# Edge attention on one core: register reads issued a run ahead, two-batch one-hots, wider windows, and 13 more gathered columns taken on chip

## The chip, the core and the metric

The kernel runs on one core of a Trainium2 chip. The metric is device time in microseconds (us) of one launch; the time shown is the median of three runs. TensorE is called PE, its weight loads PEld, VectorE DVE, ScalarE ACT, GpSimd POOL and SyncE SP, as in the profile.

## The reference, cut to what matters

A graph layer over N = 6250 nodes and E = 206,250 edges sorted by destination, 8 heads of 16:

```python
Qh, Kh, Vh = h @ WQ, h @ WK, h @ WV          # 6250 x 128, seen as 8 heads of 16
Eh = edge_attr @ WE                          # 206250 x 128
score = einsum('ehd,ehd,ehd->eh', Kh[src], Qh[dst], Eh) / 4
score = exp(clip(score, -5, 5))              # one number per edge and head
wV = segment_sum(Vh[src] * score[:, :, None], dst)
Z  = segment_sum(score, dst)
out = layernorm(h + wV / (Z + 1e-6))
```

## The kernel before, in words

**Tiles and batches.** The edges are cut into NT = 1612 tiles of 128; 4 tiles are a batch (`cut_batches`, L62), 401 full batches and five short ones at the end. From batch 12 on the order of every engine is written out by hand: what the loop at L591 emits is the order in which each engine's instructions stand (`manual_schedule`, L593).

**The rows of K and V.** At the start `table` (L270) computes K and V of all nodes and writes them to the HBM table `kv`, and keeps x transposed on chip in `xT_sb`. `gather` (L410) then fetches, per tile, the 128 rows `kv[src]` by one indirect DMA that POOL issues (L419); up to 12 batches of gathered rows (`GB`) are kept, and the first gather of batch b waits for PE's expansion of batch b - lag(b), where `lag` (L360) falls from 12 to 3.

**Column tiles.** For some tiles the rows are not gathered: their 128 source nodes' columns of x are copied out of `xT_sb` into a tile `xcol` and multiplied by the K and V weights (`project_columns` L394, `place_columns` L404). `column_tiles` (L73) picks 163 last-of-batch tiles, 3 in every 7 batches. Of the 128 columns of such a tile ACT copies 88 (L392, one per instruction, in 11 runs of 8) and DVE 40 (L389, two per instruction, in 5 runs of 8, so 4 instructions a run). The addresses are numbers in `col_at`; before each run `columns` (L369) loads its 8 addresses into registers of that engine (L382, one TENSOR_LOAD, an instruction that the engine's instruction queue carries out itself; the profile shows it as DVEq and ACTq) and the run's copies follow directly. How many runs are due at a batch follows from a linear rule (L375). DVE's runs all stand in one place, after `messages` (L636).

**One batch.** Iteration b emits, for DVE: `kq` of batch b-1 (L481, K rows times Q rows), the one-hot of batch b+2 (`stage_0`, L449, 128 x 4 x 64), `kqe` of b-1 (L484, times the edge projection), the transposed one-hot of b+2 (`stage_0t`, L459, 126 x 512 in bf16), the sum per head `sc` (L487), `msg` of b-2 (L525), the column runs (L389), the clip of `sc` (L490). In four places `fill` (L583) puts one instruction of a Q block (L301) or of a layernorm (L741) between these. For PE: `eps` (L471, edge projection of b, which waits until `kqe` of b-1 has read the one buffer), `qps` (L474, Q rows by the transposed one-hot), blocks that are complete (`finps`, L510), `agg` (L547, sums per node by the one-hot, batch b-2), and the column product (L401). For ACT: half of its column runs, the copy of a complete block (`fin`, L520), the placing of a column product (L408), the two exps of b-1 (L497, L498), the other column runs, the copy of a finished window's sums (L553).

**Windows.** `agg` sums 128-row one-hots: 8 successive tiles share a window, whose two halves of 4 tiles sit in rows 0 to 63 and 64 to 127; two windows share a PSUM tile and are copied out together. When all windows of a pair of 128-node blocks are there, `finish` (L513) adds them with shifted identities on PE (`add_windows`), ACT copies the result to `fin`, and the layernorm goes through `fill`, from `rz` (L749) on.

**Second half of the destinations.** `from_window(1)` (L183), at batch 30, loads `dB_sb` by DMA and DVE's next instruction (L191) uses it.

Of the kernel before, what the change touches and what calls it, by code (L numbers as in the profile page):

```python
# [9 lines left out]
F32 = mybir.dt.float32  # L10
# [7 lines left out]
P = 128  # L18
# [3 lines left out]
B = 4  # L22
G = 4
HW = 64
HALF = 16
# [8 lines left out]
OHB = (3, 5)  # L34
# [17 lines left out]
COLP = (7, 3)  # L52
COLA = (8, 11)
COLV = (8, 5)
COLL = 8
RING = 4096
SUMS = 8
# [22 lines left out]
def pair_of(t):  # L80

    return (t // (2 * G), t // G % 2) if t < LAST else (NT, 1)


def pair_start(k):

    return (2 * k * G * N + NT // 2) // NT - DRIFT


def window_start(t):  # L90
    k, half = pair_of(t)
    return QL * P + HW if k == NT else pair_start(k) + HALF * half

# [7 lines left out]
def edge_attention(ctx: ExitStack, tc: tile.TileContext, x, xT, srcT, srcC, dstT, dstB, dst0, bnd, lo, eaT,  # L101
# [25 lines left out]
    halves = [[cp.tile([P, B, P], F32, name=f"onehot{h}{i}") for i in range(OHB[h])] for h in range(2)]  # L127
# [11 lines left out]
    with ExitStack() as fast:  # L139
# [8 lines left out]
        nc.vector.tensor_scalar(shift[:HW], io_i[:HW], 0, None, op0=ALU.is_equal)  # L148
        nc.vector.tensor_scalar(shift[HW:], io_i[HW:], HALF - HW, None, op0=ALU.is_equal)
        nc.vector.tensor_scalar(ident, io_i[:, P:2 * P], 0, None, op0=ALU.is_equal)  # L150
        for h in range(2):
            for tl in halves[h]:
                nc.vector.memset(tl[:, :, HW - HW * h:P - HW * h], 0.0)
        nc.vector.tensor_copy(iota_f, io2)
        dB_sb = [ip.tile([P, WT * P], I32, name="dB_sb", bufs=1)]
        nc.scalar.dma_start(dB_sb[0][:min(P, NJ)], dstB[:min(P, NJ)])
# [189 lines left out]
        def load_chunk(c):  # L346
            if c in chunks or c * CH >= NT:
                return
            n = min(CH, NT - c * CH) * P
            tl = ep.tile([P, CH * P], F32, name="ea")  # L350
            nc.sync.dma_start(tl[:, :n], eaT[:, c * CH * P:c * CH * P + n])
            chunks[c] = tl
# [12 lines left out]
        used = [0, 0]  # L365

        copied, projected = {}, []

        def columns(eng, b, share=1.0):  # L369
# [6 lines left out]
            while copied.get(engine, 0) < min(due, len(col_batches) * runs):  # L376
                k, j = divmod(copied.get(engine, 0), runs)
                copied[engine] = copied.get(engine, 0) + 1
                if k not in col_tiles:
                    col_tiles[k] = wp.tile([P, P], F32, name="xcol", bufs=4)  # L380
                to, j = col_tiles[k].bitcast(U8), first + j * size
                at = nc.values_load_multi_w_load_instructions(  # L382
                    col_at[k % col_half:k % col_half + 1, k // col_half, j:j + size], engines=(engine,),
                    min_val=XT_AT, max_val=XT_AT + 8 * (N - 1) + 4,
                    skip_runtime_bounds_check_because="edges name nodes")[1]
# [57 lines left out]

        def stage_0(b):
            t0, n = batches[b][0], len(batches[b])
            half = pair_of(t0)[1]
            oh = halves[half][used[half] % OHB[half]]
            used[half] += 1
            nc.vector.tensor_tensor(oh[:, :n, HW * half:HW * half + HW],  # L449
                                    iota_p[:, None, :].to_broadcast([P, n, HW]),  # L450
                                    rel[:, t0:t0 + n, None].to_broadcast([P, n, HW]), op=ALU.is_equal)
            st8[b] = oh, None

        def stage_0t(b):
            t0, n = batches[b][0], len(batches[b])
            oh = st8[b][0]
            ohT = wp.tile([QROWS, B * P], BF16, name="onehotT", bufs=AHEAD + 2)
# [3 lines left out]
            st8[b] = oh, ohT  # L461
# [39 lines left out]
        def windows(q):  # L501

            return [(k, pair_start(k) - q * P) for k in range(min(NT, LAST + 2 * G - 1) // (2 * G))
                    if -HW - HALF < pair_start(k) - q * P < P]

        def add_windows(ps, q, first, stop):

            parts = windows(q)
            for i, (k, s) in enumerate(parts):
                nc.tensor.matmul(ps, shift[:, P - s:2 * P - s], sums[k // 2][:, k % 2],  # L510
                                 start=first and i == 0, stop=stop and i == len(parts) - 1)

        def finish(j):  # L513
# [6 lines left out]
            nc.scalar.copy(fin, ps)  # L520
            pending.append(layernorm(nc, sp, fin, xbs.pop(q), out, q, 2, stores))
# [8 lines left out]
        def stage_c(b):  # L530
            n, g, oh, m = st8.pop(b)
            for i in range(n):
                t = batches[b][i]
                k, half = pair_of(t)
# [5 lines left out]
                u = k if final else k // 2  # L540
                first = u not in aggs
                if first:
                    aggs[u] = psA.tile([P, 2, MW], F32, name="agg")
                    if final:
                        add_windows(aggs[u][:, 0], QL, True, False)
                tail = k == NT if t == NT - 1 else pair_of(t + 1)[0] != k
                nc.tensor.matmul(aggs[u][:, 0 if final else k % 2], oh[:, i, :], m[:, i, :],  # L547
                                 start=not final and t % (2 * G) == 0, stop=tail)
                if tail and final:
                    norms.insert(0, layernorm(nc, sp, aggs.pop(u)[:, :1], xbs.pop(QL), out, QL, 1, stores))  # L550
                elif tail and (k % 2 == 1 or t == LAST - 1):
                    sums[u] = sp.tile([P, 2, MW], F32, name="sum", bufs=SUMS)
                    nc.scalar.copy(sums[u][:, :k % 2 + 1], aggs.pop(u)[:, :k % 2 + 1])  # L553
                    while len(finished) < QL // 2 and all(v // 2 <= u for v, _ in windows(2 * len(finished) + 1)):
# [262 lines left out]
```

## Time and profile before

| | |
|---|---|
| median of three runs | 1858.12 us (1856.61 to 1858.39) |
| the profiled execution: its own time | 1862.53 us |
| the profiled execution: span, first to last instruction | 1860.7 us |
| granted TensorE clock, mean | 0.922 |
| gathers: from the table kv, from x | 1401, 48 |
| column tiles | 163 |
| moved by DMA | 378.43 MB, mean 203 GB/s |

The page's group lines give line, engine, operation, output<-input, number, busy us and mean ns of one, then the idle time of the engine just before these instructions and what ended it. "Issue" there means that the profile shows nothing that the engine waited for. DVE's and ACT's instructions overlap their neighbours by some 0.08 us, so a mean duration is longer than the step from one start to the next.

### The profile page before, as it was taken

How to read it: one execution, taken by the hardware profiler on the slowest of the kernel's cores; microseconds unless marked ns; L12 is line 12 of the kernel's file. 1: busy time of each engine (PE TensorE's matmuls, PEld its weight loads, DVE VectorE, ACT ScalarE, POOL GpSimd, SP SyncE). 2: the span in 40 equal slices, each digit the busy share in tenths (PEclk: the TensorE clock that was granted, in tenths of full speed). 3: DMA queues.
4: the chain of work that ended last, by engine and by line, in shares of the span. 5: the costliest groups of instructions: out<-in, count | busy, mean ns of one | idle time of the engine just before them, and what ended most of it. 6: DMA issues, size and time to landing. Idle time of an engine off the chain costs nothing.

```text
span 1860.7 us, 48856 instructions
## 1 busy us (share of the span) xinstructions
PE 1330.8 (72%) x9376; PEld 1158.3 (62%) x9376; DVE 1680.8 (90%) x6913; ACT 1632.9 (88%) x15519; POOL 1385.7 (74%) x1456
## 2 busy tenths in 40 slices
PE   6887577677776777776776776766777767666776
PEld 4776466566665666665665665656666656656665
DVE  5589799999999999999999999989998999998987
ACT  2339689899999999999999999999999999998992
POOL 6777677777777777777777777777777777777774
PEclk7998799899999999999999899998898999998998
DMA  9776657667776576677677667667766676667662
GB/s 299 213 230 196 180 173 214 199 203 205 209 215 204 178 238 202 187 219 224 192 210 227 190 198 222 198 185 217 215 207 181 204 222 192 194 197 226 204 195 70
DMA packets 171231, 378.43 MB, mean 203 GB/s; under 512 B 58622, under 2 KB 84556, under 8 KB 170918
## 3 DMA queue, kind: packets, MB, share of 16 engines
q0 software_dynamic: 68768, 186.80, 34.6%
q1 hardware_dynamic: 101010, 187.38, 33.1%
q14 instruction: 237, 1.94, 0.3%
q8 instruction: 76, 1.25, 0.3%
q10 hardware_dynamic: 1140, 1.06, 0.2%
HBM read 360.30 MB, written 14.81 MB: 202 GB/s over the span
## 4 chain that ended last, share of the span: by engine, by line
DVE 43%; PE 11%; DMA 11%; issue 6%; DVEq 5%; POOL 4%; ACT 2%; ACTq 0%; POOLq 0%
DMA kvrows<-kv,src 11%; DVE kqe L484 8%; DVE kq L481 8%; DVE xcol L389 7%; DVE sc L487 5%; DVE msg L525 5%; DVEq L382 5%; PE eps L471 4%; DVE onehot L449 4%; POOL kvrows L419 4%; DVE onehotT L459 3%; PE finps L510 3%; PE agg L547 2%; DVE sc L490 1%; ACT xcol L392 1%
## 5 line engine op out<-in xcount | busy, mean ns | idle before, releaser
L419 POOL DMA_INDIRECT kvrows<-kv,src x1401 | 1338.9, 956 | 434.4 <-issue 305.5
L392 ACT COPY xcol<-xT_sb 128x4 uint8 x14344 | 1442.5, 191 | 44.7 <-issue 37.3
L471 PE MATMUL eps<-we_sb,ea 128*128 128x128 f32 x3224 | 489.5, 298 | 456.6 <-issue 224.0
L471 PEld LDWEIGHTS eps<-we_sb,ea 128*128 128x128 f32 x3224 | 425.8, 205 | 549.8 <-issue 458.4
L547 PE MATMUL agg<-msg,onehot 128*128 128x136 f32 x3224 | 533.9, 313 | 35.8 <-DVE msg L525 24.9
L547 PEld LDWEIGHTS agg<-msg,onehot 128*128 128x128 f32 x3224 | 454.5, 211 | 88.9 <-DVE msg L525 86.5
L389 DVE TENSOR_TENSOR xcol<-xT_sb 128x8 uint8 x3260 | 298.8, 159 | 25.1 <-issue 22.8
L481 DVE TENSOR_TENSOR kq<-kvrows,qps 128x512 f32<-128x512 f32 x406 | 274.4, 676 | 46.5 <-DMA kvrows<-kv,src 25.3
L484 DVE TENSOR_TENSOR kqe<-kq,eps 128x512 f32<-128x512 f32 x406 | 272.9, 672 | 2.5 <-PE eps L471 2.1
L525 DVE TENSOR_TENSOR msg<-kvrows,exp_p 128x512 f32<-128x512 f32 x406 | 272.2, 670 | 2.7 <-ACT exp_p L498 2.6
L487 DVE TENSOR_REDUCE sc<-kqe 128x32 f32<-128x512 f32 x406 | 271.1, 668 | 0.4
L449 DVE TENSOR_TENSOR onehot<-iota_p,dst_sb 128x256 f32<-128x256 f32 x406 | 167.3, 413 | 3.2 <-PE agg L547 3.2
L474 PE MATMUL qps<-qw,onehotT 126*128 126x128 bf16 x1612 | 168.8, 229 | 0.0
L459 DVE TENSOR_SCALAR onehotT<-relb,node 126x512 bf16<-126x512 bf16 x406 | 148.6, 367 | 4.6 <-PE qps L474 3.8
L497 ACT ACTIVATE msg<-sc 128x32 f32<-128x32 f32 x406 | 92.8, 229 | 66.0 <-DVE sc L490 61.7
L474 PEld LDWEIGHTS <-onehotT 126*128 126x128 bf16 x1612 | 134.8, 104 | 8.7
L401 PE MATMUL colkv<-wkv_sb,xcol 128*128 128x256 f32 x326 | 108.7, 418 | 0.0
L490 DVE TENSOR_SCALAR sc<-sc 128x32 f32<-128x32 f32 x406 | 82.2, 202 | 0.2
L510 PE MATMUL finps<-sum,shift 128*128 128x136 f32 x640 | 81.0, 285 | 0.0
L510 PEld LDWEIGHTS finps<-sum,shift 128*128 128x128 f32 x640 | 77.5, 194 | 0.0
L498 ACT ACTIVATE exp_p<-sc 128x32 f32<-128x32 f32 x406 | 74.0, 182 | 0.0
L419 POOL DMA_INDIRECT kvrows<-x,src x48 | 45.9, 955 | 20.6 <-issue 12.8
(76 smaller groups left out, 569.1 us busy)
## 6 DMA issues: line engine op xcount, KB each, us to landing
ea<-eaT SPq DMA_DIRECT2D x201, 512.0 KB
relb<-relD SPq DMA_DIRECT2D x100, 504.0 KB
kvrows<-kv,src POOLq DMA_INDIRECT x1401
qw<-qs SPq DMA_DIRECT2D x202, 31.5 KB
kv<-kvst SPq DMA_DIRECT2D x12, 512.0 KB
qs<-qst SPq DMA_DIRECT2D x48, 96.0 KB
xst<-xT SPq DMA_DIRECT2D x12, 256.0 KB
xb<-x SPq DMA_DIRECT2D x24, 128.0 KB
```

The lines of the kernel that those rows point to most:

```text
L389: eng.tensor_tensor(to[:, 4 * (j + c):4 * (j + c) + 8], *both, op=ALU.bitwise_or)
L392: copy(to[:, 4 * (j + c):4 * (j + c) + 4], xT_bytes[:, ds(at[c] - XT_AT, 4)])
L419: ins = nc.gpsimd.indirect_dma_start(out=g[:k, i, :f], out_offset=None, in_=rows, in_offset=bass.IndirectOffsetOnAxis(ap=src_col(t)[:k], a ...
L449: nc.vector.tensor_tensor(oh[:, :n, HW * half:HW * half + HW], iota_p[:, None, :].to_broadcast([P, n, HW]), rel[:, t0:t0 + n, None].to_bro ...
L471: nc.tensor.matmul(pe[:, i, :], ea[:, i * P:i * P + P], we_sb, start=True, stop=True)
L474: expanded[b] = nc.tensor.matmul(pq[:, i, :], ohT[:, i * P:i * P + P], loaded[t0 // WT], start=True, stop=True)
L481: nc.vector.tensor_tensor(t0[:, :n], g[:, :n, :D], pq[:, :n], op=ALU.mult)
L484: nc.vector.tensor_tensor(t1[:, :n], t0[:, :n], pe[:, :n], op=ALU.mult)
L487: nc.vector.tensor_reduce(sc[:, :n], t1[:, :n].rearrange("p b (h d) -> p b h d", h=H), axis=AX.X, op=ALU.add)
L510: nc.tensor.matmul(ps, shift[:, P - s:2 * P - s], sums[k // 2][:, k % 2], start=first and i == 0, stop=stop and i == len(parts) - 1)
L525: nc.vector.tensor_tensor(m[:, :n, :D].rearrange("p b (h d) -> p b h d", h=H), g[:, :n, D:].rearrange("p b (h d) -> p b h d", h=H), exp_p[ ...
L547: nc.tensor.matmul(aggs[u][:, 0 if final else k % 2], oh[:, i, :], m[:, i, :], start=not final and t % (2 * G) == 0, stop=tail)
```

## The change

- **Addresses.** `columns` keeps a list of loaded runs per engine: before a run's copies it loads the addresses of the run after it, and the copies use the registers that were loaded a run earlier.
- **Columns.** 6 column tiles in every 13 batches (`COLP`); the code's `column_tiles` gives 176 of them (the change's title says 175), against 163. ACT copies 80 columns of each (10 runs of 8), DVE 48 (6 runs). DVE's runs stand after `messages` in even iterations; in odd iterations half are due after `kq` and half after `kqe`, where no one-hot stands any more. `xcol` has 5 buffers instead of 4.
- **One-hots.** One DVE instruction makes the one-hots of two batches (128 x 8 x 64), one the transposed ones (126 x 1024), in every second iteration.
- **Windows.** A window is 16 tiles: its four parts of 4 tiles lie 16 rows apart, which the start of the slice taken from the one-hot buffer does. There are 101 windows' sums of 136 columns, each copied out by itself, and 185 products with a shifted identity in `finish` instead of 320.
- **Blocks.** ACT's copy of a complete block stands behind the two exps of the iteration instead of ahead of them.
- **dB_sb.** The loads go into a buffer of the ring of edge tiles (`ea`). The first is issued when `from_window(0)` first runs instead of among the first loads of ACT's queue; at the second three iterations pass between the load and its first use.

In emitted order, an even iteration of DVE is kq, one-hot, kqe, transposed one-hot, sc, msg, 2 or 3 times (load, 4 copies), clip; an odd one is kq, 1 or 2 times (load, 4 copies), kqe, 1 or 2 times (load, 4 copies), sc, msg, clip; with the fill instructions between as before.

```diff
+QUAD = 4
+STEPS = 16
-OHB = (3, 5)
+OHB = 5
-COLP = (7, 3)
-COLA = (8, 11)
-COLV = (8, 5)
+COLP = (13, 6)
+COLA = (8, 10)
+COLV = (8, 6)
+XCOLS = 5
-SUMS = 8
+SUMS = 9
...
         def from_window(i):
-            if i == len(dB_sb):
-                dB_sb.append(ip.tile([P, WT * P], I32, name="dB_sb", bufs=1))
-                nc.sync.dma_start(dB_sb[i][:k], dstB[a:a + k])
-            d = dB_sb[i]
+            d = ep.tile([P, WT * P], I32, name="dB_sb", tag="ea")
+            (nc.sync if i else nc.scalar).dma_start(d[:k], dstB[a:a + k])
+            if i:
+                yield
+                yield
+                yield
...
         def columns(eng, b, share=1.0):
-            while copied.get(engine, 0) < min(due, len(col_batches) * runs):
+            total = len(col_batches) * runs
+            while copied.get(engine, 0) < min(due, total):
...
-                at = nc.values_load_multi_w_load_instructions(
-                    col_at[k % col_half:k % col_half + 1, k // col_half, j:j + size], engines=(engine,),
+                known = addresses.setdefault(engine, [])
+                while len(known) < 2 and fetched.get(engine, 0) < total:
+                    kf, jf = divmod(fetched.get(engine, 0), runs)
+                    fetched[engine] = fetched.get(engine, 0) + 1
+                    jf = first + jf * size
+                    known.append(nc.values_load_multi_w_load_instructions(
+                        col_at[kf % col_half:kf % col_half + 1, kf // col_half, jf:jf + size], engines=(engine,),
...
+                at = known.pop(0)
...
+        def together(b):
+            t0 = batches[b][0]
+            n = len(batches[b])
+            if n == B and b + 1 < nbat and len(batches[b + 1]) == B and t0 % (2 * B) == 0:
+                return [b, b + 1]
+            return [] if n == B and t0 % (2 * B) else [b]
         def stage_0(b):
-            nc.vector.tensor_tensor(oh[:, :n, HW * half:HW * half + HW],
+            nc.vector.tensor_tensor(tl[:, HW:].rearrange("p (t n) -> p t n", n=P)[:, :n, :HW],
...
+            for i in group:
+                st8[i] = tl, HW + (batches[i][0] - t0) * P - window_of(batches[i][0])[1], None
         def stage_0t(b):
-            ohT = wp.tile([QROWS, B * P], BF16, name="onehotT", bufs=AHEAD + 2)
+            ohT = wp.tile([QROWS, 2 * B * P], BF16, name="onehotT", bufs=3)
...
         def finish(j):
-            nc.scalar.copy(fin, ps)
-            pending.append(layernorm(nc, sp, fin, xbs.pop(q), out, q, 2, stores))
+            def copied_out():
+                nc.scalar.copy(fin, ps)
+                pending.append(layernorm(nc, sp, fin, xbs.pop(q), out, q, 2, stores))
+            blocks_out.append(copied_out)
...
-                    aggs[u] = psA.tile([P, 2, MW], F32, name="agg")
+                    aggs[k] = psA.tile([P, 1, MW], F32, name="agg")
...
-            if b + AHEAD < nbat:
+            if b + AHEAD < nbat and together(b + AHEAD):
                 stage_0(b + AHEAD)
+            elif b < nbat:
+                columns(nc.vector, b, 0.5)
             fill()
             next(steps, None)
-            if b + AHEAD < nbat:
+            if b + AHEAD < nbat and together(b + AHEAD):
                 stage_0t(b + AHEAD)
+            elif b < nbat:
+                columns(nc.vector, b, 1.0)
...
                 weigh(b - 1)
+            while blocks_out:
+                blocks_out.pop(0)()
```

More of the change, by code (lines that the diff above doesn't have):

```diff
@@ L126, in edge_attention @@
     ident = cp.tile([P, P], F32, name="ident")
-    halves = [[cp.tile([P, B, P], F32, name=f"onehot{h}{i}") for i in range(OHB[h])] for h in range(2)]
+    onehots = [cp.tile([P, HW + 2 * B * P], F32, name=f"onehot{i}") for i in range(OHB)]
     cnt_i = cp.tile([1, 1], I32, name="cnt_i")
@@ L364, in edge_attention @@
         col_tiles, xT_bytes = {}, spread.bitcast(U8)
-        used = [0, 0]
+        used = [0]
         copied, projected = {}, []
+        addresses, fetched = {}, {}
         def columns(eng, b, share=1.0):
@@ L460, in stage_0t @@
                                     op0=ALU.is_equal)
-            st8[b] = oh, ohT
+            for i in group:
+                tl, at, _ = st8[i]
+                k = (batches[i][0] - t0) * P
+                st8[i] = (tl, at), ohT[:, k:k + len(batches[i]) * P]
         def stage_a(b, g):
```

82 lines of the change are left out of this document (40 added, 42 removed).

## The prediction, made before the changed kernel was run

> **What bounds the kernel now.** First the page, then one line at a time over a stretch in the middle (362 to 1087 us): how fast POOL issues gathers there, and how fast DVE starts batches (one `kq` each).
>
> ```profile
> span 1860.7 us, 48856 instructions
> PE 1330.8 (72%) x9376; PEld 1158.3 (62%) x9376; DVE 1680.8 (90%) x6913; ACT 1632.9 (88%) x15519; POOL 1385.7 (74%) x1456
> ...
> L419 POOL DMA_INDIRECT kvrows<-kv,src x1401 | 1338.9, 956 | 434.4 <-issue 305.5
> L419 POOL DMA_INDIRECT kvrows<-x,src x48 | 45.9, 955 | 20.6 <-issue 12.8
> L419 POOL DMA_INDIRECT kvrows<-kv,src x577: 942/949/1186, 361.1 to 1086.3; - x193
> L481 DVE TENSOR_TENSOR kq<-kvrows,qps x169: 647/680/689, 362.3 to 1086.9; 128x512 f32<-128x512 f32 x169
> L481 DVE TENSOR_TENSOR kq<-kvrows,qps x170: 409/681/690, 1086.9 to 1836.1; 128x512 f32<-128x512 f32 x169, 128x256 f32<-128x256 f32 x1
> 362.00:1087.00 725.00, 526.27 (x3812) 460.96 (x3812) 688.53 (x2920) 696.95 (x6797) 549.15 (x577) 0.94 0.70 206
> ```
>
> POOL is only 74% busy on the page, yet it is full: 577 gathers started between 361.1 and 1086.3, 725.2/576 = 1.259 us each, 0.95 of work and some 0.30 of issue that no gather escapes. A batch has 4 - 3/7 = 3.571 gathers, so POOL passes **4.50 us a batch**. DVE in that stretch takes (1086.9 - 362.3)/168 = **4.313 us a batch**: it is catching up on rows that POOL had gathered ahead. From 1086.9 on it takes 749.2/169 = 4.433: it has caught up and waits for POOL. So POOL sets the end of this run, and DVE is only 0.19 us a batch (4%) behind it as the next limit. ACT (696.95 of 725 us, the fourth group in the stretch's row, in which PE, PEld, DVE, ACT and POOL stand in order) is as full as DVE.
>
> Without POOL, DVE would start its 337 steps from 362.3 at 4.313 each, and the stretch behind the first short batch would follow: 362.3 + 337 x 4.313 + (1860.7 - 1836.1) = **1840**. That is the DVE line before the change; POOL's is the measured 1860.7.
>
> **POOL after.** 1612 - 176 = 1436 gathers instead of 1449: 13 x 1.259 = 16.4 us less, **1844**. A batch costs POOL 4 - 6/13 = 3.538 gathers, 4.45 us. That is the whole gain on offer, if DVE stays below 4.45.
>
> **DVE after: the work.** One batch of before, from start to start:
>
> ```profile
> 1010.09 0.68 DVE L481 TENSOR_TENSOR kq<-kvrows,qps 128x512 f32<-128x512 f32 x1
> 1010.68 0.42 DVE L449 TENSOR_TENSOR onehot<-iota_p,dst_sb 128x256 f32<-128x256 f32 x1
> 1011.02 0.68 DVE L484 TENSOR_TENSOR kqe<-kq,eps 128x512 f32<-128x512 f32 x1
> 1011.61 0.35 DVE L459 TENSOR_SCALAR onehotT<-relb,node 126x512 bf16<-126x512 bf16 x1
> 1011.88 0.68 DVE L487 TENSOR_REDUCE sc<-kqe 128x32 f32<-128x512 f32 x1
> 1012.47 0.68 DVE L525 TENSOR_TENSOR msg<-kvrows,exp_p 128x512 f32<-128x512 f32 x1
> 1013.07 0.73 DVE L389 TENSOR_TENSOR xcol<-xT_sb 128x8 uint8 x8
> 1013.72 0.17 DVE L490 TENSOR_SCALAR sc<-sc 128x32 f32<-128x32 f32 x1
> 1013.80 0.67 DVE L481 TENSOR_TENSOR kq<-kvrows,qps 128x512 f32<-128x512 f32 x1
> ```
>
> And the groups of lines with their shapes kept apart:
>
> ```profile
> L449 DVE TENSOR_TENSOR onehot<-iota_p,dst_sb 128x256 f32<-128x256 f32 x401 | 166.0, 415 | 3.2 <-PE agg L547 3.2
> L459 DVE TENSOR_SCALAR onehotT<-relb,node 126x512 bf16<-126x512 bf16 x401 | 146.9, 367 | 4.6 <-PE qps L474 3.8 <-DMA relb<-relD 0.7
> L449 DVE TENSOR_TENSOR onehot<-iota_p,dst_sb 128x128 f32<-128x128 f32 x3 | 0.9, 284 | 0.0
> L459 DVE TENSOR_SCALAR onehotT<-relb,node 126x128 bf16<-126x128 bf16 x2 | 0.5, 246 | 0.0
> ```
>
> - Columns: a column instruction is (1013.72 - 1013.07)/8 = 0.08 us. Runs a batch go from 5 x 3/7 = 2.14 to 6 x 6/13 = 2.77: 0.63 x 4 x 0.08 = **+0.20 us a batch**.
> - One-hot: 256 against 128 elements, 415 against 284 ns, is 1.02 ns an element; it steps 0.34 now, so the double one steps 0.34 + 0.26 = 0.60 for two batches: -0.04 a batch.
> - Transposed: 512 against 128 elements, 367 against 246 ns, 0.315 ns an element; steps 0.27 now, 0.27 + 0.16 = 0.43 for two: -0.055 a batch.
>
> Net +0.105 a batch, over 382 batches with columns **+40 us**. The sizes 512 and 1024 stand in no row; with no saving from joining it is +76, with the second halves free (0.17 and 0.135 a batch) -40; I take the slopes, `kq` with 512 elements also stepping 0.59.
>
> **DVE after: the address loads.** This is the step that decides. A load of eight addresses takes DVE's queue 0.6 us. What stands behind it on the same queue waits, needed or not:
>
> ```profile
> L382 DVEq TENSOR_LOAD <-col_at x2: 595/596/597, 1011.7 to 1012.6; - x2
> L657 DVEq TENSOR_LOAD <-cnt_i x1: 311/311/311, 431.2 to 431.2; - x1
> 431.22 0.29 DVE L311 TENSOR_TENSOR qst<-qr,qst 128x128 bf16<-128x128 f32 x1
> 431.80 0.69 DVE L481 TENSOR_TENSOR kq<-kvrows,qps 128x512 f32<-128x512 f32 x1 [0.29 <-DVE qst L311]
> L389 DVE TENSOR_TENSOR xcol<-xT_sb 128x8 uint8 x3260 | 298.8, 159 | 25.1 <-issue 22.8
> ```
>
> The rows are those of the two load lines in short stretches, then two of the timeline, then the page's group. The load of L657 (from 431.2, 0.311 long) fetches a number that nothing uses until the end; still `kq` behind it started at 431.80, after the load, with DVE idle for 0.29. So I take a load to hold the queue. Then an address read one run ahead is no sooner in effect: the load of run k+1 now stands in front of the copies of run k and holds them just as long. A rule that speaks against the change: section "Sequencer Loop" of "Perfetto Trace Analysis" in the Trainium skill has a control instruction executed by the queue's own code, while an engine's instruction is only pushed on; by it the early address gains nothing, and the row agrees. What counts is how much DVE work is queued ahead while a load runs. The first load starts as `kqe` ends (1011.70, load at 1011.7), the next 0.85 later: copies come 0.6, 1.45 and 2.3 after `kqe`, and 0.1 more to start. DVE itself, with transposed one-hot, sc and msg before them, reaches the first run at 1.37 and is through two at 2.02. So two runs are covered and a **third waits 2.4 - 2.02 = 0.38**. Before, 15/7 runs a batch means three in every seventh, 55 in all: 55 x 0.38 = 21, and 22.8 us of issue stand in the row.
>
> After, counted over the emitted order:
>
> - Even: 146 of the iterations have a third run after msg; the longer transposed one-hot covers 0.16: 146 x 0.22 = 32 us.
> - Odd: a run stands behind `kq` and behind `kqe`, each only 0.59 long. One load (0.6) just fits. A second run in the same place (74 times behind kq, 73 behind kqe) comes at 0.6 + 0.85 + 0.1 = 1.55, while DVE is through at 0.59 + 0.32 = 0.91: 0.64 idle, less the lead of the queue, which I know from no row (0 to 0.4; I take 0.2): 147 x 0.45 = 66 us.
>
> 98 less 23 is **+75 us** (between 40, with full lead and the fill instructions covering, and 125, with none).
>
> **DVE after: waits that go or come.**
>
> ```profile
> DVE rz L749 <- ACT fin L520: 39.3, 24, 3.6
> DVE wq L191 <- DMA dB_sb<-dstB: 11.2, 1, 11.2
> ACT fin L520 <- PE finps L510: 31.5, 23, 4.4
> ...
> L510 PE MATMUL finps<-sum,shift 128*128 128x136 f32 x640 | 81.0, 285 | 0.0
> ```
>
> The waits (total, times, longest) and one group. DVE's layernorm waits for `fin`, ACT for PE's products. A product is two of the 640 matmuls, 81.0/640 = 0.127 us each; 135 fewer products over 24 blocks let PE be done 135 x 2 x 0.127/24 = 1.4 us sooner, and ACT does the exps meanwhile. `fin` now stands behind the exps, so a little is left: -34 (0 to -39). The wait for `dB_sb` goes, three iterations being 13 us: -11 (0 to -11). New: in an odd iteration `kq` follows `kqe` sooner (one run 0.32, sc 0.59, msg 0.60, clip 0.08: 1.6 us), and needs `qps`, which follows `eps`, which waits for `kqe`:
>
> ```profile
> 1011.84 1.13 PE L471 MATMUL eps<-we_sb,ea 128*128 128x128 f32 x8 [1.32 <-DVE kqe L484]
> 1012.81 0.39 PE L474 MATMUL qps<-qw,onehotT 126*128 126x128 bf16 x4
> ```
>
> Here qps ended at 1013.20, 1.5 after kqe: it fits by 0.1 where PE is undisturbed. I take +10 (0 to 35). The first `dB_sb` load goes out later among ACT's copies at the start, but PE's table of K and V, not it, holds the first batch: 0 (-2 to 5).
>
> **ACT after.**
>
> ```profile
> L392 ACT COPY xcol<-xT_sb 128x4 uint8 x14344 | 1442.5, 191 | 44.7 <-issue 37.3
> L553 ACT COPY sum<-agg 128x272 f32<-128x272 f32 x100 | 37.6, 376 | 1.7 <-PE agg L547 1.7
> ```
>
> 176 x 80 = 14,080 copies instead of 14,344 at 1442.5/14,344 = 0.10: -27 us; half-wide sums some -10; 13 more placings +5. ACT gets lighter by 32 us of 1633 and waits on DVE instead: nothing on the path. PE's 270 fewer matmuls lie off the path but for `fin`.
>
> **The sum.** DVE's line: 1840 + 40 + 75 - 34 - 11 + 10 = **1920**, or about 4.53 us a batch; POOL's line is 1844, and the later of them sets the end. So DVE takes POOL's place and POOL begins to wait. The unchanged kernel's median lies 2.6 us under the span used here (1858.1 to 1860.7), so the forecast is 1918, 3.2% slower.
>
> **Rivals.**
>
> 1. *The queue goes on during a load that nothing behind it needs* (faster). Then the addresses are there a run early, the 98 us of load stalls are gone, and DVE's line is 1920 - 98 = 1822; POOL's 1844 decides, a median of **1842**. For it: loads in the middle of a batch lie beside busy DVE, and the one case that I have of an unneeded load (L657) is one row. Against it: that row. It decides as soon as the loads cost DVE less than 98 - (1920 - 1844) = 22 us, what they cost before. The section "DVE / Act Engine Instruction" of the same page of the Trainium skill says that an instruction that must wait does so in a wait queue, and the sequencer is free at once; by that alone loads could start long before `kqe` ends, and this rival would hold. In this trace the first load starts as `kqe` ends.
> 2. *The fill instructions and the queue's lead cover most of the stalls* (still slower). Loads cost +25, not +75: 1870, median **1867**. Against it: third runs cost their full 0.38 to 0.41 before, fills included.
> 3. *PE becomes the wait of the odd iterations.* Every odd `kq` waits a further 0.3 (PE's chain at 1.9 instead of 1.5): 190 x 0.3 = +57, of which 10 are in the sum: 1967, median **1964**. For it: eps takes longer where PE is throttled; against it, kq waited little for qps in the batch above.
> 4. *The lines end together* (several bounds low together: work +10, loads +40, fin -39): 1840; POOL 1844 again, as in 1, or with half of that between 1850 and 1862.
>
> **Chances.** Forecast with its own range 1885 to 1950: 0.66. Rival 1: 0.13. Rival 2 (1862 to 1885): 0.12. Rival 3: 0.04. Rival 4: 0.05, of which 0.03 within 0.2%. About 0.2% (3.7 us) is what a measurement can tell from no change. Faster 0.15, same 0.03, slower 0.82. The range leaves out rival 1 and rival 3 and takes in the rest: 1850 to 1950.
>
> **What would show it.** In the changed profile: kq steps of about 4.53 us over the whole middle, without a change of pace near 1087; POOL's idle before gathers far above 0.30 each and ended by qps; DVE's idle before `xcol` near 100 us, "issue" its cause; `rz` waiting for `fin` under 10 us; `wq` not waiting; the double one-hot near 676 ns and the transposed one near 530; ACT waiting for the clip. I am wrong if `xcol` idles under 30 us (the loads do go on beside), if POOL still passes a gather every 1.26 us to the end, or if `kq` waits for `qps` by more than 30 us.

## The result, and the profile after

The changed kernel takes **1948.3 us** (median of 6 runs, 1940.7 to 1956.3) against 1858.3 of the kernel before (6 runs, 1856.6 to 1862.9): a ratio of **1.048**, 95% interval 1.046 to 1.050. The forecast was 1918, with 1885 to 1950 as its own range: it had the sign and the mechanism, and two thirds of the rise, and the measured time lies just inside its upper bound. The profiled execution took 1944.7 us, with a span of 1943.0 and a mean granted clock of 0.902.

First the page of the kernel after: its heads, and the groups that answer to those shown of before.

```profile
span 1943.0 us, 48929 instructions
...
PE 1345.3 (69%) x9130; PEld 1167.6 (60%) x9130; DVE 1743.3 (90%) x7478; ACT 1633.6 (84%) x15268; POOL 1372.0 (71%) x1443
...
L399 DVE TENSOR_TENSOR xcol<-xT_sb 128x8 uint8 x4224 | 406.7, 162 | 87.3 <-issue 79.1
```

Over the span (+82.3 us) DVE is busy 62.5 us more and idle 19.8 us more (199.7 against 179.9). The small number hides two large ones. Ahead of the column copies the idle time grew from 25.1 to 87.3 us, by "issue", so the profile shows nothing that they waited for; other waits went. These are they, in the waits of DVE (total, times, longest):

```profile
DVE xcol L399 <- issue: 79.1, 219, 1.1
DVE qst L309 <- PE qrows L305: 26.1, 33, 2.3
DVE kq L507 <- PE qps L500: 16.2, 24, 1.1
...
DVE wq L192 <- DMA dB_sb<-dstB: 7.9, 2, 6.6
...
DVE rz L785 <- ACT fin L550: 3.3, 4, 1.5
...
DVE kq L507 <- DMA kvrows<-kv,src: 1.8, 4, 0.6
```

Three of the same waits in the kernel before:

```profile
DVE kq L481 <- DMA kvrows<-kv,src: 25.3, 22, 2.8
...
DVE qst L308 <- PE qrows L304: 6.8, 13, 1.3
...
DVE kq L481 <- PE qps L474: 5.1, 15, 0.6
```

The last line of after says who sets the end now: `kq` hardly waits for gathered rows any more (1.8 us instead of 25.3). The rows of `kq` and of the gathers in the stretch used in the prediction and in the one behind it (number, then first and last start) agree:

```profile
L507 DVE TENSOR_TENSOR kq<-kvrows,qps x156: 644/683/691, 363.4 to 1084.6; 128x512 f32<-128x512 f32 x156
L429 POOL DMA_INDIRECT kvrows<-kv,src x540: 940/946/1208, 362.3 to 1086.2; - x180
L507 DVE TENSOR_TENSOR kq<-kvrows,qps x154: 650/682/690, 1088.9 to 1798.4; 128x512 f32<-128x512 f32 x154
```

And the busy time of PE, PEld, DVE, ACT and POOL in the two stretches, with the granted clock, DMA share and GB/s behind them:

```profile
362.00:1087.00 725.00, 499.15 (x3438) 436.77 (x3437) 666.57 (x2937) 648.74 (x6190) 514.59 (x540) 0.90 0.66 193
1087.00:1800.00 713.00, 493.77 (x3414) 430.79 (x3413) 657.42 (x2911) 640.03 (x6104) 509.11 (x535) 0.90 0.67 194
```

A batch now takes (1084.6 - 363.4)/155 = **4.65 us** (4.53 was forecast), and 709.5/153 = 4.64 later: one pace, without the change of pace that the kernel before has near 1087. Before, it took 4.31 while DVE caught up and 4.43 when POOL held it. Gathers come every 723.9/539 = 1.343 us instead of 1.259: POOL waits, DVE sets the end. DVE's own busy share (666.57 of 725 us) is lower than before too: its line got longer by gaps, not by work alone.

How a lost half microsecond looks, in the timeline of DVE of the kernel after (start, length; idle before in brackets):

```profile
1000.32 0.40 DVE L399 TENSOR_TENSOR xcol<-xT_sb 128x8 uint8 x4
1000.63 0.68 DVE L510 TENSOR_TENSOR kqe<-kq,eps 128x512 f32<-128x512 f32 x1
1001.23 0.40 DVE L399 TENSOR_TENSOR xcol<-xT_sb 128x8 uint8 x4
1002.02 0.41 DVE L399 TENSOR_TENSOR xcol<-xT_sb 128x8 uint8 x4 [0.40 <-issue]
1002.35 0.67 DVE L513 TENSOR_REDUCE sc<-kqe 128x32 f32<-128x512 f32 x1
...
1007.00 0.72 DVE L399 TENSOR_TENSOR xcol<-xT_sb 128x8 uint8 x8
1007.92 0.40 DVE L399 TENSOR_TENSOR xcol<-xT_sb 128x8 uint8 x4 [0.20 <-issue]
```

The loads on DVE's queue from 1000.5 to 1002.5, in the rows of their line:

```profile
L391 DVEq TENSOR_LOAD <-col_at x2: 609/610/611, 1000.5 to 1001.3; - x2
```

The second run behind `kqe` starts at 1002.02. Its addresses were known before; but the load that started at 1001.3, for the run after it, stands ahead of it, takes 0.61 and ends at 1001.93. The first run's copies were through at 1001.62: 0.40 us idle. At 1007.92 a third run behind `msg` loses 0.20. These are the two cases that the prediction had priced at 0.45 and 0.22.

The whole trace says the same. Of the 219 gaps by issue ahead of DVE's copies, 209, with 75.0 of their 79.1 us, end 0.09 us after the end of a load on DVE's queue. And by place, the 87.3 us of idle time are 30.7 ahead of the second runs behind `kq` (73 of them), 27.8 ahead of the second runs behind `kqe` (73), 20.7 ahead of the third runs behind `msg` (147), and 8.0 ahead of all others.

### The profile page after: what moved, and what is told of

It reads as the page before. It is cut to its first block, busy times and chain, and to the rows that moved or that the text cites. A ratio compares the mean times of both kernels' runs of the same rounds, so it can differ in the third digit from the quotient of the medians.

```text
span 1943.0 us, 48929 instructions
## 1 busy us (share of the span) xinstructions
PE 1345.3 (69%) x9130; PEld 1167.6 (60%) x9130; DVE 1743.3 (90%) x7478; ACT 1633.6 (84%) x15268; POOL 1372.0 (71%) x1443
## 4 chain that ended last, share of the span: by engine, by line
DVE 49%; DMA 13%; PE 10%; issue 9%; DVEq 7%; POOL 5%; ACT 1%; ACTq 0%; POOLq 0%; SPq 0%
DMA kvrows<-kv,src 12%; DVE xcol L399 11%; DVE kqe L510 8%; DVE kq L507 7%; DVE sc L513 7%; DVEq L391 7%; POOL kvrows L429 5%; DVE msg L557 4%; PE agg L577 4%; DVE onehot L469 4%; PE eps L497 3%; DVE onehotT L482 3%; DVE sc L516 2%; DMA dB_sb<-dstB 1%; PE colkv L411 1%
## 5 line engine op out<-in xcount | busy, mean ns | idle before, releaser
L429 POOL DMA_INDIRECT kvrows<-kv,src x1388 | 1325.0, 955 | 528.6 <-issue 330.3
L402 ACT COPY xcol<-xT_sb 128x4 uint8 x14080 | 1432.4, 190 | 92.5 <-issue 83.1
L497 PE MATMUL eps<-we_sb,ea 128*128 128x128 f32 x3224 | 503.9, 304 | 444.5 <-DVE kqe L510 314.2
L497 PEld LDWEIGHTS eps<-we_sb,ea 128*128 128x128 f32 x3224 | 440.5, 210 | 541.8 <-issue 414.1
L577 PE MATMUL agg<-msg,onehot 128*128 128x136 f32 x3224 | 555.6, 322 | 114.2 <-DVE msg L557 106.8
L577 PEld LDWEIGHTS agg<-msg,onehot 128*128 128x128 f32 x3224 | 474.9, 219 | 167.4 <-DVE msg L557 147.1
L399 DVE TENSOR_TENSOR xcol<-xT_sb 128x8 uint8 x4224 | 406.7, 162 | 87.3 <-issue 79.1
L507 DVE TENSOR_TENSOR kq<-kvrows,qps 128x512 f32<-128x512 f32 x406 | 275.2, 678 | 28.3 <-PE qps L500 16.2
L469 DVE TENSOR_TENSOR onehot<-iota_p,dst_sb 128x512 f32<-128x512 f32 (+2 forms) x206 | 138.3, 672 | 2.0 <-PE agg L577 2.0
L482 DVE TENSOR_SCALAR onehotT<-relb,node 126x1024 bf16<-126x1024 bf16 (+2 forms) x206 | 103.0, 501 | 4.9 <-DMA relb<-relD 3.5
L524 ACT ACTIVATE exp_p<-sc 128x32 f32<-128x32 f32 x406 | 73.7, 182 | 0.0
L418 ACT COPY kvrows<-colkv 128x256 f32<-128x256 f32 x176 | 63.7, 362 | 0.3 <-PE colkv L411 0.3
L411 PEld LDWEIGHTS colkv<-wkv_sb,xcol 128*128 128x128 f32 x352 | 63.4, 221 | 0.2 <-ACT xcol L402 0.2
## 6 DMA issues: line engine op xcount, KB each, us to landing
qw<-qs SPq DMA_DIRECT2D x202, 31.5 KB
```

Of the source, the lines that this page charges most:

```text
L399: eng.tensor_tensor(to[:, 4 * (j + c):4 * (j + c) + 8], *both, op=ALU.bitwise_or)
L402: copy(to[:, 4 * (j + c):4 * (j + c) + 4], xT_bytes[:, ds(at[c] - XT_AT, 4)])
L411: nc.tensor.matmul(pk, col_tiles.pop(k), wkv_sb, start=True, stop=True)
L429: ins = nc.gpsimd.indirect_dma_start(out=g[:k, i, :f], out_offset=None, in_=rows, in_offset=bass.IndirectOffsetOnAxis(ap=src_col(t)[:k], a ...
L469: nc.vector.tensor_tensor(tl[:, HW:].rearrange("p (t n) -> p t n", n=P)[:, :n, :HW], iota_p[:, None, :].to_broadcast([P, n, HW]), rel[:, t ...
L497: nc.tensor.matmul(pe[:, i, :], ea[:, i * P:i * P + P], we_sb, start=True, stop=True)
```

## The experiments

**Theory 1** (the prediction's): a load holds everything behind it on its engine's queue for 0.6 us, so its price is what the instructions ahead of it don't cover; reading one run ahead puts it in front of copies that need nothing from it. **Theory 2**: the place of the load is of no matter; the gaps belong to the copies, to the registers, or to what DVE waits for anyhow. The first four kernels ran on a chip where the kernel before takes 1859 us.

**a_once: DVE reads once.**

```diff
-                while len(known) < 2 and fetched.get(engine, 0) < total:
+                while len(known) < (1 if eng is nc.vector else 2) and fetched.get(engine, 0) < total:
...
-                at = known.pop(0)
+                at = known[0] if eng is nc.vector else known.pop(0)
```

> The kernel after, with VectorE reading the eight addresses of its first run alone and using them for all its runs; the other reads of addresses on VectorE are left out, so that VectorE's columns are those of other nodes; the copies are as many as before, and ScalarE is as in the kernel after. Theory 1 (reads hold the queue): the 80 us of idle time by issue ahead of VectorE's column copies go, below 15 us are left, and the time falls by 65 to 95 us to 1853 to 1883. Theory 2 (the gaps belong to the copies, or to what the engine waits for anyhow): idle time and time as after, 1948 within 10.

Measured: 1838.2 us, ratio 0.990 (0.988 to 0.991); 110 us less than the kernel after, more than Theory 1 had. The group of the copies in this run, the rows of `kq` and of the gathers in the stretch, and a wait of DVE:

```profile
L399 DVE TENSOR_TENSOR xcol<-xT_sb 128x8 uint8 x4224 | 378.8, 156 | 0.2 <-issue 0.2
```

```profile
L507 DVE TENSOR_TENSOR kq<-kvrows,qps x171: 646/676/690, 361.5 to 1086.1; 128x512 f32<-128x512 f32 x171
L429 POOL DMA_INDIRECT kvrows<-kv,src x577: 942/946/1234, 361.5 to 1086.2; - x193
```

```profile
DVE kq L507 <- DMA kvrows<-kv,src: 22.4, 23, 3.5
```

The same 4224 copies cost 0.2 us of idle time instead of 87.3, and 27.9 us less busy time. DVE passes a batch in (1086.1 - 361.5)/170 = 4.262 us, POOL a gather in 724.7/576 = 1.258 as before the change, and `kq` waits for rows again. With the reads of DVE left out, the whole loss is gone, and POOL is the limit again, 20 us earlier than before. This kernel copies the same eight columns over and over; that this alone makes its copies cheap is ruled out by a_behind below, which reads every address and whose copies are busy for 380.2 us.

**a_noahead: no reading ahead.**

```diff
-                while len(known) < 2 and fetched.get(engine, 0) < total:
+                while len(known) < 1 and fetched.get(engine, 0) < total:
```

> The kernel after without the reading ahead: each run's addresses are read directly ahead of its own copies, as in the kernel before; all else as after. Theory 1: a read holds the queue in either case, so reading one run ahead gains nothing: 1948 within 6, and the idle time ahead of VectorE's column copies stays at 80 to 100 us. Theory 2 (the queue goes on while a read that nothing needs is under way, so the change did gain by it): the copies now have to wait for their own read, some 0.5 us more for each of the second and third runs, 1980 or more.

Measured: 1950.9 us, ratio 1.051 (1.049 to 1.053), 80.1 us in 223 gaps ahead of the copies (79.1 in 219 after). Reading one run ahead is worth nothing here, on either engine: ScalarE's gaps are 83.4 us without and 83.1 us with it. Copies whose addresses were read a run earlier wait for the load ahead of them as long as copies that need it; rival 1 of the prediction falls.

**a_behind: each load behind the copies of the run before it.**

```diff
-                while len(known) < 2 and fetched.get(engine, 0) < total:
...
+                ahead(1)
                 at = known.pop(0)
...
                     copy(to[:, 4 * (j + c):4 * (j + c) + 4], xT_bytes[:, ds(at[c] - XT_AT, 4)])
+                ahead(1)
```

Here `ahead(1)` loads the next run's addresses if none are held.

> The kernel after, with each read of eight addresses put behind the eight copies of the run before it instead of ahead of them, on VectorE and on ScalarE. Theory 1 (a read holds its engine's queue, and read ahead it stands in front of copies that need nothing from it): the idle time ahead of the column copies on VectorE, 87 us in the kernel after, falls below 20 us, ScalarE's (83 us by issue) by more than half, and the time falls by 75 to 100 us until GpSimd's gathers bind, to 1845 to 1870. Theory 2 (the order of read and copies is of no matter; the copies themselves or their registers cost the idle time): 1948 within 5.

Measured: 1879.4 us, ratio 1.012 (1.009 to 1.015): 69 us less than after, a little less than the 75 to 100 of Theory 1, and not 1948. The gaps ahead of ScalarE's copies fell from 83.1 to 1.5 us. The idle time ahead of DVE's copies went to 1.5 us as well, but a part of it went elsewhere; the group of the copies, three waits of DVE and a piece of its timeline:

```profile
L403 DVE TENSOR_TENSOR xcol<-xT_sb 128x8 uint8 x4224 | 380.2, 157 | 1.5 <-issue 0.9
```

```profile
DVE sc L518 <- DVE xcol L403: 16.7, 49, 0.6
DVE kqe L515 <- DVE xcol L403: 10.4, 29, 0.5
DVE y L808 <- DVE xcol L403: 4.2, 11, 0.7
```

```profile
1002.28 0.70 DVE L403 TENSOR_TENSOR xcol<-xT_sb 128x8 uint8 x8
1003.34 0.58 DVE L810 TENSOR_SCALAR h<-h,mv,y 128x128 f32<-128x128 f32 x1 [0.37 <-DVE xcol L403]
```

The load behind the last copies of a place now holds what follows them: `kqe`, `sc`, a fill instruction. The trace ends such waits with the copies, since a queue's load ends no wait in this view. That is the same price at another place, and smaller: all waits of this kind add up to 43 us, about what this kernel takes longer than a_once (41 us, 37 between the profiled executions). Near 1000.3 us three runs' copies follow one another without a gap; the three loads that stand behind those runs started at 998.8, 999.7 and 1000.5, the last of them with ten copies still to run, which it could not hold up.

**a_fin: finished blocks copied ahead of the exps, as before.**

```diff
-            blocks_out.append(copied_out)
+            copied_out()
```

> The kernel after, with the finished blocks copied ahead of the exps as in the kernel before. Theory 1 (as the prediction has it, that moving the copies took 34 us of waits out of the layer norms): the norms' idle time for the copied block comes back, 30 us or more against 3, and the time rises by 25 to 40 us to 1973 to 1988. Theory 3 (the late copy holds one of the few PSUM buffers that the query rows need too, and VectorE's 26 us of waits for those rows, 7 in the kernel before, are its price): those waits fall below 12 us, and the time rises by no more than 20 us, 1945 to 1968.

Measured: 1947.0 us, ratio 1.049 (1.046 to 1.052): no difference from 1948.3, and neither theory's waits of DVE moved. The waits of DVE, then one of ACT (31.5 us in the kernel before, 8.2 in the kernel after):

```profile
DVE qst L309 <- PE qrows L305: 22.9, 33, 2.1
...
DVE rz L785 <- ACT fin L550: 2.2, 4, 0.7
```

```profile
ACT fin L550 <- PE finps L536: 23.4, 19, 2.9
```

The layernorm's waits for the block stay away with the copy in its old place, so the late copy did not remove them. What did, the 135 products fewer or a DVE that is later by itself, was not taken apart; but in a_once, where DVE passes a batch in 4.26 us against 4.31 in the kernel before, the wait is 8.2 us against 39.3, so a later DVE is not all of it. The late copy isn't what makes `qst` wait for its rows either; that cause stays open.

**On other chips.** The remaining kernels ran on three further chips, where the kernel before takes 2540 to 2546 us instead of 1859, so they compare only with it and with the kernel after there. For that the kernel after itself was run beside the last of them. The runs on the first chip are also the earlier ones, so it is not shown that the chip is what makes the difference.

> The kernel after, nothing changed, beside the next kernel on one chip: on two chips the kernel before took 2540 to 2546 us, with some 520 us of gaps ahead of ScalarE's column copies that wait for nothing the profile shows, and the change itself was not run there. Theory 1 (there ScalarE's chain is the end, so what VectorE loses in its column runs is hidden, and ScalarE has 13 tiles more but 8 columns of each fewer): where the kernel before takes 2540, the change is 0.97 to 1.00 of it, and the edits to VectorE's columns measured there differ from it by little. Theory 2 (VectorE's gaps cost the same there): 1.03 or more. Where the kernel before takes 1859: 1948 within 6 by either.

Measured: 2462.5 us against 2545.6, ratio **0.965** (0.960 to 0.970), just below the 0.97 to 1.00 of Theory 1: there the change makes the kernel *faster*. The chain that ended last (shares by engine), the two column groups and the longest waits of the kernel after on that chip:

```profile
ACT 40%; issue 22%; DVE 11%; PE 9%; ACTq 5%; another core or an unknown queue 4%; POOL 3%; DMA 2%; DVEq 1%; SPq 0%; POOLq 0%
```

```profile
L402 ACT COPY xcol<-xT_sb 128x4 uint8 x14080 | 1503.8, 190 | 533.7 <-issue 521.3
L399 DVE TENSOR_TENSOR xcol<-xT_sb 128x8 uint8 x4224 | 412.0, 160 | 141.9 <-issue 132.0
```

```profile
ACT xcol L402 <- issue: 521.3, 1004, 1.2
DVE xcol L399 <- issue: 132.0, 328, 0.9
```

ScalarE's column copies, the same 190 ns each as on the first chip, have 1004 gaps ahead of them, 521 us in all, against 293 and 83 us. They wait for nothing that the profile shows; the loads take the same time as on the first chip (a median of 606 ns on DVE and 557 on ACT on both). Most of these gaps aren't those of the loads: on the first chip all 293 stand ahead of the first copy of a run of eight, 280 of them ending 0.07 us after a load. Here 801, with 435.8 of the 521.3 us, stand inside a run, where no load stands between the copies, as in these rows of ScalarE's timeline:

```profile
240.28 0.19 ACT L402 COPY xcol<-xT_sb 128x4 uint8 x1 [0.52 <-issue]
240.99 0.19 ACT L402 COPY xcol<-xT_sb 128x4 uint8 x1 [0.52 <-issue]
241.71 0.19 ACT L402 COPY xcol<-xT_sb 128x4 uint8 x1 [0.52 <-issue]
```

What causes them stays open. The chain says what they do: ScalarE's copies and the gaps ahead of them set the end. That DVE's gaps, even longer here, cost nothing, the next experiment shows.

**a_spread: each load behind a long instruction.** The reads are taken one at a time behind `kq`, `kqe`, `sc` and `msg` (0.67 us each), up to four runs ahead; a run's copies follow its read much later.

```diff
+AHEADV = 4
...
+            if COL0 - COLL < b < nbat:
+                read_ahead(nc.vector, AHEADV)
```

> The kernel after, with VectorE's reads taken one at a time behind kq, kqe, the reduction and the messages, up to four runs ahead, so that each read stands behind an instruction of 0.67 us that takes as long as the read; nothing is left out. Theory 1 (a read costs what the instructions ahead of it in the queue don't cover): next to none of VectorE's idle time by issue is left, nor of the idle time ahead of kqe and the reduction that the reads behind the copies brought (29 us there), and the time is that of VectorE reading once, 1838, up to 1850. Theory 2 (a read costs what it takes wherever it stands): 1879 or more.

> The same kernel again: in its first run the kernel before took 2546 us, against 1859 in the runs of the other experiments. The kernel after, with VectorE's reads taken one at a time behind kq, kqe, the reduction and the messages, up to four runs ahead; nothing is left out. Theory 1 (a read costs what the instructions ahead of it in the queue don't cover): where the kernel before takes 1859, 1838 to 1850, a ratio of 0.989 to 0.995. Theory 2 (a read costs what it takes wherever it stands): 1879 or more, a ratio of 1.011 or more.

> The kernel with VectorE's reads taken one at a time behind kq, kqe, the reduction and the messages, once more. Where the kernel before takes 1859: theory 1 (a read costs what the instructions ahead of it in the queue don't cover) 1838 to 1850, a ratio of 0.989 to 0.995; theory 2 (a read costs what it takes wherever it stands) 1879 or more. Where the kernel before takes 2540: 2465 as before, a ratio of 0.970, and by theory 1 within 25 us of the kernel after beside it.

Measured on the three chips: 2466.7, 2465.3 and 2465.6 us, ratios 0.970, 0.970 and 0.970 (0.964 to 0.976 on the last), beside the kernel after's 0.965 on the last. In the lines of DVE of the last:

```profile
L408 DVE TENSOR_TENSOR xcol<-xT_sb 128x8 uint8 x4224 | 380.6, 157 | 17.4 <-issue 12.6
L519 DVE TENSOR_TENSOR kqe<-kq,eps 128x512 f32<-128x512 f32 x406 | 273.0, 672 | 6.8 <-remote 3.3 <-PE eps L506 1.9 <-DVE kq L516 1.1
L522 DVE TENSOR_REDUCE sc<-kqe 128x32 f32<-128x512 f32 x406 | 271.3, 668 | 17.1 <-issue 5.8 <-DVE xcol L408 4.3 <-DVE y L814 3.0
```

With as many loads, just as long, 132.0 us of gaps by issue ahead of the copies became 12.6, and 31 us of busy time went with them (412.0 to 380.6), as in a_once. The time, held by ScalarE, did not move, as the expectation of after_again had it. Two things remain open. DVE's `msg` waits 208 us for ScalarE's `exp_p` in this kernel (105 in the kernel after on this chip), and such a wait may cover a load too, so the long instructions aren't shown to be all that covers the loads. And whether the kernel gives the expected 1838 to 1850 where DVE is the limit was not measured.

**a_msgcols, a_split, a_spread21.** Three more edits ran on the first of those chips, a_split on the second as well, where they cannot answer what they were for.

In a_msgcols all of VectorE's runs stand behind the messages:

```diff
-            elif b < nbat:
-                columns(nc.vector, b, 0.5)
...
-            elif b < nbat:
-                columns(nc.vector, b, 1.0)
```

In a_split the column split is that of before:

```diff
-COLP = (13, 6)
-COLA = (8, 10)
-COLV = (8, 6)
+COLP = (7, 3)
+COLA = (8, 11)
+COLV = (8, 5)
```

And a_spread21 is a_spread with a column tile every 2 batches:

```diff
-COLP = (13, 6)
+COLP = (2, 1)
```

> The kernel after, with all of VectorE's column runs behind the messages, none in the odd iterations behind kq and kqe, where the change put some of them. Theory 1 as the prediction has it (0.45 us for a second run behind kqe, 0.22 us for a third behind the messages): the second runs get cheaper by about 0.2 us and the time falls by 20 to 35 us to 1913 to 1928. Theory 2 (where the runs stand is of no matter, since each second or third run of a place waits for its read there as well): idle time ahead of the column copies 75 to 110 us, time 1948 within 10.

> The kernel after with the column split of the kernel before (7 batches for 3 column tiles, 88 columns of each by ScalarE, 40 by VectorE); one-hots of two batches, reading ahead and late block copies stay. Theory 1 (VectorE's 964 more column copies, and the reads that go with them, are what costs; the one-hots of two batches gain): VectorE's busy time falls below that of the kernel before by 30 us or more and GpSimd's gathers bind again: 1845 to 1865. Theory 2 (the two-batch one-hots and the placing cost most of it): 1890 or more.

> The same kernel again, for the same reason: the kernel after with the column split of the kernel before (40 columns of each tile by VectorE, 13 tiles fewer). Theory 1 (VectorE's 964 more column copies and the reads that go with them are what costs): where the kernel before takes 1859, GpSimd's gathers bind again at 1845 to 1865. Theory 2 (the two-batch one-hots and the placing of the copies cost most of it): 1890 or more.

> The same with a column tile every 2 batches instead of every 13/6, 15 column tiles more, so 15 gathers fewer on GpSimd and 360 copies more on VectorE, 1200 more on ScalarE. Theory 1 (with the reads covered, GpSimd's gathers at 1.255 us each bind): 10 to 19 us less than with 13/6, 1820 to 1835. Theory 3 (VectorE still binds): 20 to 35 us more than with 13/6.

| kernel | us | ratio to before (95%) | DVE's gaps by issue ahead of its copies, us |
|---|---|---|---|
| a_msgcols | 2482.3 | 0.974 (0.971 to 0.978) | 161.6 |
| a_split | 2487.2; 2492.3 | 0.976 (0.973 to 0.979); 0.982 (0.979 to 0.985) | 65.3; 62.5 |
| a_spread21 | 2534.8 | 0.996 (0.993 to 0.998) | 29.3 |

None of these times is near a number expected, since those supposed DVE or POOL at the end. What can be read: with all runs behind the messages the gaps are 161.6 us, not less than the 132.0 of the kernel after, so that standing behind the messages did not make the moved runs cheaper on this chip. On the first chip, though, the second runs of odd iterations are dearer, as Theory 1 has it: 58.5 us over 146 of them, 0.40 each, against 20.7 over 147 third runs, 0.14 each. ScalarE's 1200 further copies in a_spread21 make it busy for 111 us longer than in a_spread, and the time is 68 us longer, which agrees with ScalarE as the limit there but doesn't show it. With the old split the change keeps 1.8 to 2.4 of its 3.5 per cent, if these chips are alike; no run separates what the rest of that gain comes from.

## Why the prediction was right, and where it was short

- **POOL is full, DVE next.** Right. a_once is the change without DVE's reads, and POOL is full in it: 1838 against the 1842 of rival 1, where POOL's line decides. Of the signs that were named, POOL's idle time came in part only: 528.6 us over 1388 gathers, 0.38 each and not far above 0.30, and `qps` ended 73.7 us of it.
- **The loads decide.** Right: a load holds the queue (a_noahead, a_behind), the stalls sit where the prediction put them, and taking the loads away takes the whole loss away. Idle ahead of the copies was forecast at 98 us and is 87.3: 20.7 for the third runs instead of 32, 58.5 for the second runs of odd iterations instead of 66, and 8.0 for runs that were to cost nothing. One support of the 98 was partly luck. In the kernel before, 55 third runs at 0.38 gave 21 us and the row had 22.8 by issue; counted by place in its trace, the 25.1 us there are 14.5 for 54 third runs, 0.27 each, and 10.4 for second runs, which the prediction took as covered.
- **The size: the term of the loads was too small.** The span is 1943 against 1920, 23 us more. What goes away with the loads between the kernel after and a_once is 87.1 us of idle time ahead of the copies and 27.9 us of the copies' busy time (406.7 against 378.8), 115 us in all where the sum had 98. The 28 us the prediction had left at nothing. They are mainly lost overlap: a copy that starts behind another steps 0.08 us, but the last copy ahead of a gap lasts its full 0.16. Counted in the traces, the first copies of the 1056 runs overlap the instruction ahead of them by 50.6 us in all in the kernel after and by 81.7 in a_once, 31 us more; and 397 copies start after some idle time, of which the waits list the 219 that idled longest, so each loses some 0.08. DVE's busy time on the page points the same way: forecast +40, measured +62.5. The other 6 of the 23 us are spread over waits that no run took apart. The medians differ by 30, 1948.3 against 1918, in part because the profiled execution (1944.7) is faster than its kernel's median.
- **Everything but the loads** came out about as forecast in sum. The prediction's line without the loads is 1920 - 98 = 1822. The same sum at a_once's pace, with its 336 batches from 361.5 us to the first short one and the 21.7 us behind that, is 361.5 + 336 x 4.262 + 21.7 = 1815. That is an estimate, good to some 15 us: the same sum for the kernel after, 363.4 + 338 x 4.653 + 21.9, gives 1958, and 1943 was measured.
- **One-hots.** Right: 676 and 530 ns were forecast for the doubled ones. The groups with shapes apart have 684 and 506:

```profile
L469 DVE TENSOR_TENSOR onehot<-iota_p,dst_sb 128x512 f32<-128x512 f32 x200 | 136.6, 684 | 0.9 <-PE agg L577 0.9
L482 DVE TENSOR_SCALAR onehotT<-relb,node 126x1024 bf16<-126x1024 bf16 x200 | 101.2, 506 | 4.9 <-DMA relb<-relD 3.5 <-PE qps L500 1.4
```

- **fin, -34.** The size was right (39.3 to 3.3 us), the reason half wrong: the step "`fin` now stands behind the exps" had no part in it (a_fin). The other half, fewer products, no run shows by itself.
- **dB_sb, -11.** Right for the second load: of its 11.2 us 7.9 - 6.6 = 1.3 are left. But the first load now lets DVE wait at the start, where the prediction had `wq` not waiting, as the timeline of the kernel after has it (`wq` at 13.9 us waited for nothing before). That it was priced at nothing holds all the same: the first `kq` starts at 62.85 us, against 62.91 before.

```profile
19.18 0.16 DVE L192 TENSOR_TENSOR wq<-dB_sb,bnd_c 128x1 f32<-128x1 int32 x1 [6.61 <-DMA dB_sb<-dstB]
```

- **qps, +10:** +11.1 measured (16.2 against 5.1), right. **Not foreseen:** `qst` waits 26.1 us for its rows instead of 6.8, and the cause is open. That such errors nearly cancel in the sum of everything but the loads is luck.
- **Rivals.** 1 fell (a_noahead). 2 (fills and the lead of the queue cover most: loads +25) fell: the copies idle 62 us more than before (87.3 against 25.1), and the 219 longer gaps still are 79.1/219 = 0.36 us each. The lead that the prediction guessed at 0.2 is in the timeline: the load that began at 1001.3 found copies to run for another 0.3 us. 3 fell, `kq` waits for `qps` 16 us in all, and 4 with it, since DVE's line ends alone. By the rule cited from "Sequencer Loop" of "Perfetto Trace Analysis" in the Trainium skill the early address gains nothing, and a_noahead agrees (80.1 against 79.1 us). What the prediction drew for rival 1 from the section "DVE / Act Engine Instruction" there, that loads could start long before `kqe` ends, is not what the traces show: in the kernel after 183 of DVE's 1056 loads begin 0.04 to 0.06 us after a `kqe` has ended, and 612 follow another load within 1 us.

## What to carry to other kernels

In these runs a load of addresses cost what the work pushed ahead of it on its queue didn't cover. That its result is needed a run later bought nothing (1948.3 against 1950.9 us); standing behind the copies instead of ahead of them, it cost 69 us less. So count such a load against the instructions that stand ahead of it, and try it behind a long one: there DVE's gaps by issue ahead of its copies went from 132.0 to 12.6 us, though what that is worth where DVE is the limit was not measured. Price a gap in a row of short instructions at its idle time and one lost overlap (here 0.36 us for the longer gaps, and 0.08). And ask which engine's line is the limit on the chip at hand: the same change was 4.8% slower where VectorE's line set the end and 3.5% faster where ScalarE's did.

## What the runs showed of the hardware that was not expected

- Eight addresses take 0.61 us on DVE and 0.56 on ACT, the medians in the rows of the load line in the kernel after; with each load behind the copies (a_behind) the medians are the same:

```profile
L391 ACTq TENSOR_LOAD <-col_at x1760: 535/557/1211, 131.6 to 1910.6; - x196
L391 DVEq TENSOR_LOAD <-col_at x1056: 591/606/1049, 131.2 to 1906.5; - x176
```

- The kernel before takes 1859 us on one chip and 2540 to 2546 on three others, the kernel after 1948 on the first and 2462 on one of the others. Of the kernel after there are traces of both. ScalarE's and DVE's copies, the gathers (955 and 953 ns) and the loads last as long on either; the gaps ahead of ScalarE's short copies are more (293 and 1004), the granted clock is lower (0.90 and 0.77), and PE's products take longer (304 and 348 ns for `eps`). Which of these comes first, no run shows.
